# Two scan chunks a step instead of three in a MetaFormer kernel with selective scans

## The chip, the cores and the metric

The kernel runs on one NeuronCore of a Trainium2 chip, as one launch. The metric is the device time of that core in microseconds (us), the median over several executions. Everything is float32.

## The reference

An image batch of 4 x 384 channels x 32 x 32 positions goes through two layers, each with a token mixer and a feed-forward part. Both mixers are selective scans (state-space models). In layer 0 the 1024 positions of an image are read in four directions (rows, columns, and both backwards); in layer 1 in one direction, but with 768 channels. What costs the time is this recurrence, for each channel `d` and each of 16 states `n`:

```python
dA = jnp.exp(dtt[..., None] * A)
h = h * dA + (dtt * ut)[..., None] * bt[:, :, None, :]
y = jnp.einsum('bkdn,bkn->bkd', h, ct)
```

`dt` is a softplus of a low-rank projection, `bt` and `ct` are projections of the input that have one row per state and position, and `A` is negative. Around the scans lie layer norms, a small feed-forward part as a Kronecker product (layer 0), input and output projections, a causal convolution of four taps and a SiLU gate (layer 1), and at the end a layer with four experts, of which each token takes two.

## The kernel before

The scan layers and the expert layer run one after the other. In `conv_layers`, work is divided into **passes**. A pass is one image, one direction (layer 0) or one group of 384 channels (layer 1), and one half of the positions, T = 512 columns. Layer 0 has 8 passes an image, layer 1 has 4: 48 passes for four images. Of the two passes over the halves of one sequence, the first starts from zero and keeps its last states (`keep_state`), the second starts from these.

Within a pass there are 384 channels x 16 states, so 48 scans of 128 partitions x 512. A partition holds one channel and one state: the upper 64 partitions hold state 2m, the lower 64 state 2m + 1, of the same 64 channels. `dts` and `dtus` hold dt and dt x u doubled that way, 64 channels to a chunk, six chunks to a pass. They are filled by DMAs from `dt` and `dtu` (`prep_pass`). A **step** takes three of the six chunks (`part` 0 or 1) and one pair of states (m = 0 to 7): 16 steps a pass, 768 in all. A step consists of:

- the loads of the rows for b and c, two DMAs of 64 partitions each into the rings `bts` and `cts` of three tiles (`load`, L849), issued on SP's queue;
- one product on POOL, `s = dtus x b`, 128 x 1536 (`times_b`, L855), into the ring `ss` of five tiles;
- three decays on ACT, `da = exp(a x dt)`, into three PSUM banks `das`, bank x for chunk x (`decay`, L861);
- three scans on DVE (`scan`, L870). A scan writes over `da` in PSUM or over `s` in SBUF;
- the products with c: for scans that ended in PSUM on DVE (`times_c`, L902), for those in SBUF on POOL (`times_c_pool`, L913). `share[i]` says how many of the three stay with DVE: 1, 2 or 3;
- three matmuls on PE that add the two states of a channel and sum over the steps into `acc` (`add`, L889). With `both` as 128 x 64 weights, each writes 64 partitions, the upper or the lower half of the array's columns by the chunk's number. Chunks 0 and 1 of a step are issued as one entry, chunk 2 as an entry of its own.

At the end of a pass `gather` takes `acc` into the result (L472 to L485, L680).

Nothing of this order is found by hardware: the class `Plan` plays the engines through with fixed costs, while it emits the instructions. Main streams (the steps) have fixed orders for each engine; **side jobs** (layer norms, projections, convolution, feed-forward, softplus, one serial chain of them) are put into the streams where a main instruction is not due, and `choose` says which goes first. `split` sets `share[i]` from how far ahead POOL is. `LOAD` (3.0 us) stands for a DMA; SP is taken to be free again after 0.1 us. Each engine then executes its list in order, with semaphores between engines.

Side jobs on ACT that need another function table reload it and go back (`SWITCH`): the softplus of each pass (L393), GELU (L495, L551) and SiLU (L638, L704).

After the scan layers, `moe_layer` keeps PE busy with the experts (L1200, L1212).

Of the kernel before, what the change touches and what calls it, by code (L numbers as in the profile page):

```python
# [17 lines left out]
P = 128  # L18
# [6 lines left out]
T = 512  # L25
# [193 lines left out]
def conv_layers(ctx, tc, ins, x2, const):  # L219
# [34 lines left out]
    dts = tiles(2, [P, NC, T], "dts")  # L254
    dtus = tiles(2, [P, NC, T], "dtus")
# [3 lines left out]
    NSR, NBR, NCR = 5, 3, 3  # L259
    ss = tiles(NSR, [P, NC, T], "s")  # L260
    bts = tiles(NBR, [P, T], "bt")
    cts = tiles(NCR, [P, T], "ct")
    state = sp.tile([P, NS, NC], F32, name="state")
# [4 lines left out]
    das = tiles(NC, [P, T], "da", pool=ps_1)  # L268
# [98 lines left out]

    def until(*keys):

        while not all(k in plan.end for k in keys):  # L370
            yield None
        return max(plan.end[k] for k in keys)

    def prep_pass(q, p, h, u, u_view):


        nr = q["rank"]
        for c in range(NC):
            pd = yield from ps.take(True)
            yield PE, 0.95  # L380
            nc.tensor.matmul(  # L381
                pd,
                lhsT=q["dtw"][QROW : QROW + nr, c * P : (c + 1) * P],
                rhs=q["xd"][QROW : QROW + nr, cols(h)],
                start=True,
                stop=True,
            )
            bias = pv(q["dtb"], q["c0"] + c, 1)
            yield ACT, 0.65
            nc.scalar.activation(dt[:, c, :], pd, AF.Identity, bias=bias)  # L390
            ps.give(pd)
        yield ACT, 1.45 + SWITCH
        nc.scalar.activation(dt, dt, AF.Softplus)  # L393
        exp_set()
        for c in range(NC):
            yield POOL, 1.35
            nc.gpsimd.tensor_tensor(u_view(dtu[:, c, :]), u_view(dt[:, c, :]), u[:, c], ALU.mult)
        for part in range(2):
            before = 0.0
            if p:  # L400
                before = yield from until(("scan", NS * (p - 1) + 8 * part + 7, 2))
            for to, of in ((dts[part], dt), (dtus[part], dtu)):
                yield SP, LOAD, before
                for side in range(2):

                    mine = [x for x in range(NC) if (3 * part + x) % 2 == side]
                    chunks = [(3 * part + x) // 2 for x in mine]
                    for k in range(2):
                        nc.sync.dma_start(
                            out=to[k * HP : (k + 1) * HP, mine[0] : mine[-1] + 1 : 2, :],  # L410
                            in_=of[side * HP : (side + 1) * HP, chunks[0] : chunks[-1] + 1, :],
                        )
            plan.end["pass", p, part] = plan.now + LOAD + 2.0
# [419 lines left out]
    steps = [(p, n) for p in range(len(passes)) for n in range(NS)]  # L833
# [11 lines left out]
    def load(i, of, ring):  # L845
        p, part, m = place(i)
        for k in range(2):
            row = of + 2 * m + k
            nc.sync.dma_start(  # L849
                out=ring[i % len(ring)][k * HP : (k + 1) * HP, :],  # L850
                in_=quad(p)["rows"][row : row + 1, cols(passes[p][4])].partition_broadcast(HP),
            )

    def times_b(i):
        nc.gpsimd.tensor_tensor(ss[i % NSR], dtus[place(i)[1]], rep(bts[i % NBR]), ALU.mult)  # L855

    def decay(i, x):
        p, part, m = place(i)
        q = quad(p)
        g = 2 * q["c0"] + 3 * part + x  # L860
        nc.scalar.activation(das[x], dts[part][:, x, :], AF.Exp, scale=q["a"][:, g, m : m + 1])  # L861

    def scan(i, x):
        p, j = steps[i]
        _, _, _, _, _, first, rev = passes[p]
        way = slice(None, None, -1) if rev else slice(None)
        s = ss[i % NSR][:, x, way]
        d = das[x][:, way]
        in_psum = x < share[i] if x else True
        nc.vector.tensor_tensor_scan(  # L870
            d if in_psum else s, d, s, 0.0 if first else state[:, j, x : x + 1], ALU.mult, ALU.add
        )
        if not in_psum:
            plan.skip.add(("mult", i, x))
            plan.end["da free", i, x] = plan.free[DVE]

    def keep_state(i, of):

        p, j = steps[i]
        at = 0 if passes[p][6] else T - 1  # L880
        for x in (0, 1) if of == 0 else (2,):
            src = das[x] if x < share[i] else ss[i % NSR][:, x, :]
            nc.vector.tensor_copy(state[:, j, x : x + 1], src[:, at : at + 1])  # L883

    def add(i, xs):
        _, part, m = place(i)
        for x in xs:
            c, side = divmod(3 * part + x, 2)
            nc.tensor.matmul(  # L889
                acc[side * HP : (side + 1) * HP, c, :],  # L890
                lhsT=both,
                rhs=ss[i % NSR][:, x, :],
                start=m == 0,
                stop=m == NS // 2 - 1,
            )
# [5 lines left out]
    def times_c(i, x):  # L901
        nc.vector.tensor_tensor(ss[i % NSR][:, x, :], das[x], cts[i % NCR], ALU.mult)  # L902
        plan.end["split", i] = 0.0
        plan.end["part", i, x] = plan.end["da free", i, x] = plan.end["mult", i, x]
        if x == 2:
            plan.end["c", i] = plan.end["mult", i, 2]
        elif share[i] == NC:
            plan.skip.add(("c", i))

    def times_c_pool(i):  # L910
        m = share[i]
        s = ss[i % NSR]
        nc.gpsimd.tensor_tensor(s[:, m:, :], s[:, m:, :], rep(cts[i % NCR], NC - m), ALU.mult)  # L913
        for x in range(m, NC):
            plan.end["part", i, x] = plan.end["c", i]

    STEP, C1, SPARE = 4.8, 1.24, 6.0
    share = dict.fromkeys(range(N), 2)
    main, gathers, decays, bs, cs, bl, cl = ([] for _ in range(7))
    adds = [[], []]  # L920
    AT = (0.0, 1.18, 3.6)
    for i in range(N):
        p, part, m = place(i)
        first = passes[p][5]
        after = ("state", i, 1) if first else ("scan", i, 2)
        ring = [("add", i - NSR, k) for k in range(2)] if i >= NSR else []
# [6 lines left out]
                [rows] + ([("mult", i - NCR, 0), ("part", i - NCR, 1), ("c", i - NCR)] if i >= NCR else []),  # L933
# [3 lines left out]
        bs.append(Op(("b", i), 3.42, [("pass", p, part), ("bt", i), *ring], lambda i=i: times_b(i)))  # L937
        for x in range(NC):
            free = [("da free", i - 1, x)] if i else []
            decays.append(Op(("da", i, x), 0.63, [("pass", p, part), *free], lambda i=i, x=x: decay(i, x)))  # L940
        for x in (0, 1, "state 0", "mult 0", "mult 1", 2, "state 1", "mult 2"):
            if isinstance(x, int):
                cost = 1.12 if first else 1.18
                op = Op(("scan", i, x), cost, [("da", i, x), ("b", i)], lambda i=i, x=x: scan(i, x))
            elif x.startswith("state"):
                k = int(x[-1])
                op = Op(("state", i, k), 0.14 - 0.07 * k, [], lambda i=i, k=k: keep_state(i, k))
                if not first:
                    continue
            else:  # L950
                k = int(x[-1])
                op = Op(("mult", i, k), 0.62, [("ct", i)], lambda i=i, k=k: times_c(i, k))
            main.append(op)
        cs.append(Op(("c", i), C1, [("ct", i), after, ("split", i)], lambda i=i: times_c_pool(i)))
        wait = [("gather", p - 1)] if m == 0 and p else []
        for k, xs in enumerate(((0, 1), (2,))):
            adds[k].append(
                Op(("add", i, k), 0.95, [("part", i, x) for x in xs] + wait, lambda i=i, xs=xs: add(i, xs))
            )
        if i % NS == NS - 1:  # L960
            gathers.append(
                Op(("gather", p), 2.0, [("add", n, k) for n in (i - 8, i) for k in range(2)], lambda p=p: gather(p))
            )

    def needed(plan, i, x):
# [4 lines left out]
        what, j, k = op.key  # L970
        y = AT[k] if what == "scan" else (2.36, 2.98, STEP)[k] if what == "mult" else (2.36, STEP)[k]
# [7 lines left out]
    def pool_choice(plan, mains, side):  # L979
# [3 lines left out]
        if 0 in by:  # L983
            t, op = by[0]
            d = plan.head(DVE, 1)
            late = (d.key[1] if d else N) - op.key[1] >= 2
# [14 lines left out]
    def split(plan, i, start):  # L1001
# [3 lines left out]
        if ahead - waiting < C1:  # L1005
            return NC
        return 1 if ahead - waiting > SPARE else 2

    def choose(plan, e, mains, side):
        if e == POOL:  # L1010
            return pool_choice(plan, mains, side)
        if e == DVE:
            for n, (t, k, op) in enumerate(mains):
                if op.key[0] == "scan" and op.key[2] == 1:
                    i = op.key[1]
                    share[i] = split(plan, i, t + 2.4)
                    plan.streams[POOL][0][i].cost = (0.0, 2.3, C1, 0.0)[share[i]]
# [7 lines left out]
        if e == ACT:  # L1025
# [3 lines left out]
            due = needed(plan, head.key[1], AT[head.key[2]]) - head.cost - LAG  # L1029
# [5 lines left out]
        if e == PE:  # L1035
            d, a = plan.head(DVE, 1), plan.head(PE, 1)
            behind = (d.key[1] if d else N) - (a.key[1] if a else N)
            if behind > 2 and best[0] <= start:
# [7 lines left out]
        {DVE: [gathers, main], ACT: [decays], POOL: [cs, bs], PE: adds, SP: [bl, cl]}, jobs, choose  # L1046
# [280 lines left out]
```

## Time and profile before

| what | us |
|---|---|
| runs shown | 6753.74, 6752.0, 6747.33 |
| median | 6752.0 |
| profiled execution, its own time | 6755.91 |
| its span in the profile | 6754.0 |
| last scan ends, from the span's start | about 4470 |
| DVE busy | 4145.4 (61%) |
| POOL busy | 4080.2 (60%) |
| ACT busy | 2735.4 (41%) |
| PE busy (overlapping matmuls counted once) | 5601.9 (83%) |

Shares over the whole span mean little, since two stages with different limits follow each other: up to about 4473 us the scans, from there on the end of the last side jobs and the expert layer. The profile names a group of instructions by its line, engine, operation and tiles, then gives their number, the time they kept the engine busy, the mean of one in ns, and the idle time just ahead of them with what ended it. A row `A <- B` of the waits is: A's engine stood idle until B was done; total us, number, longest.

### The profile page before, as it was taken

The page shows a single profiled execution, that of the slowest core. Times are in us where ns is not written, and L with a number is a line of the kernel's source. Part 1 is how long each engine was busy: PE and PEld are TensorE (multiplying, and loading weights), DVE is VectorE, ACT ScalarE, POOL GpSimd, SP SyncE. Part 2 cuts the span into 40 slices and gives each one's busy share as a digit, 9 for nine tenths or more (in the row PEclk, how much of TensorE's full clock was granted, in tenths as well). Part 3 has the DMA queues.
Part 4 walks back from the last instruction along what each step waited for, and adds up shares of the span by engine and source line. Part 5 has one row for each costly group of instructions (what it writes and reads, how often), then busy time and mean ns, then how long its engine had stood idle before and what let it go on. Part 6 is the DMA issues. An engine that isn't in the chain of part 4 may idle for free. (4 is left out here: it accounts for less than half of the span.)

```text
span 6754.0 us, 47474 instructions
## 1 busy us (share of the span) xinstructions
PE 5601.9 (83%) x12352; PEld 1929.1 (29%) x12352; DVE 4145.4 (61%) x5421; ACT 2735.4 (41%) x3911; POOL 4080.2 (60%) x1735
## 2 busy tenths in 40 slices
PE   6666789767777876878886897767899999999999
PEld 1111123112122211222221222223444444444444
DVE  6999989998889999899999885951100000000000
ACT  4444565555455645555555554432211111111111
POOL 6999888998889888999899875950000000000000
PEclk8787889887888988888887888888999999999999
DMA  4444444444445444445444433422000000000000
GB/s 130 143 140 143 138 119 141 143 134 124 133 139 159 136 132 139 130 144 157 144 142 138 118 109 106 148 88 105 0 0 0 28 0 8 21 0 0 10 14 14
DMA packets 413489, 644.55 MB, mean 95 GB/s; under 512 B 75104, under 2 KB 119200, under 8 KB 413216
## 3 DMA queue, kind: packets, MB, share of 16 engines
q1 hardware_dynamic: 413216, 641.52, 31.6%
q8 instruction: 97, 1.59, 0.1%
q14 instruction: 176, 1.44, 0.1%
HBM read 468.77 MB, written 21.50 MB: 73 GB/s over the span
## 5 line engine op out<-in xcount | busy, mean ns | idle before, releaser
L855 POOL TENSOR_TENSOR s<-dtus,bt 128x1536 f32<-128x1536 f32 x768 | 2640.6, 3447 | 177.6 <-PE acc L889 94.6
L889 PE MATMUL acc<-s,both 128*64 128x512 f32 x4608 | 2030.3, 742 | 838.1 <-POOL s L913 547.2
L861 ACT ACTIVATE da<-dts,a 128x512 f32<-128x512 f32 x2304 | 1511.2, 683 | 1469.2 <-DVE s L902 1305.7
L1226 POOL TENSOR_TENSOR xb<-xb,yg 128x1536 f32<-128x1536 f32 x32 | 118.8, 3712 | 1834.3 <-DVE yg L1223 1775.4
L1223 DVE SCALAR_TENSOR_TENSOR yg<-py,pvt,gate 128x512 f32<-128x512 f32 x96 | 66.2, 746 | 1848.8 <-PE py L1200 1846.6
L913 POOL TENSOR_TENSOR s<-s,ct 128x512 f32<-128x512 f32 (+1 forms) x673 | 1044.8, 1554 | 207.6 <-DVE state L883 54.4
L889 PEld LDWEIGHTS acc<-s,both 128*64 128x64 f32 x4608 | 483.7, 156 | 2323.9 <-POOL s L913 985.7
L1200 PE MATMUL py<-hid,w 128*128 128x512 f32 x2304 | 1046.2, 592 | 1.5 <-DVE yg L1223 1.5
L1212 PE MATMUL ph<-tb,w 128*128 128x512 f32 x2304 | 1046.3, 592 | 0.0
L870 DVE TENSOR_TENSOR_SCAN da<-da,s 128x512 f32<-128x512 f32 x736 | 871.4, 1219 | 169.3 <-POOL s L855 101.0
L870 DVE TENSOR_TENSOR_SCAN da<-da,state,s 128x512 f32<-128x512 f32 x720 | 889.3, 1273 | 100.0 <-ACT da L861 90.3
L902 DVE TENSOR_TENSOR s<-da,ct 128x512 f32<-128x512 f32 x1456 | 944.0, 682 | 10.9 <-DMA ct<-rows 6.2
L1216 ACT ACTIVATE hid<-ph,pvt 128x512 f32<-128x512 f32 x384 | 263.9, 687 | 1523.2 <-PE ph L1212 1516.9
L1200 PEld LDWEIGHTS py<-hid,w 128*128 128x128 f32 x2304 | 437.7, 190 | 553.9 <-issue 550.4
L1212 PEld LDWEIGHTS ph<-tb,w 128*128 128x128 f32 x2304 | 438.0, 190 | 552.2 <-issue 551.9
L870 DVE TENSOR_TENSOR_SCAN s<-da,state,s 128x512 f32<-128x512 f32 x432 | 550.4, 1274 | 15.8 <-ACT da L861 15.8
L870 DVE TENSOR_TENSOR_SCAN s<-da,s 128x512 f32<-128x512 f32 x416 | 503.8, 1211 | 18.1 <-ACT da L861 17.9
L591 PE MATMUL ps<-u,w 128*128 128x512 f32 x576 | 294.8, 660 | 35.9 <-DMA w<-in_w_in_dram 29.0
L381 PE MATMUL ps<-xd,dtw 12*128 12x512 f32 (+1 forms) x288 | 188.8, 749 | 32.7 <-ACT dt L390 24.5
L543 PE MATMUL ps<-t,w 32*128 32x512 f32 x192 | 148.4, 904 | 40.8 <-DMA w<-in_w_fc_dram 38.6
L591 PEld LDWEIGHTS ps<-u,w 128*128 128x128 f32 x576 | 114.9, 209 | 219.1 <-issue 171.9
L724 PE MATMUL ps<-yx,w 128*128 128x512 f32 x288 | 144.6, 655 | 38.9 <-DMA w<-in_w_out_dram 36.4
(134 smaller groups left out, 3278.1 us busy)
## 6 DMA issues: line engine op xcount, KB each, us to landing
bt<-rows SPq DMA_DIRECT2D x1536, 128.0 KB, 3.0
ct<-rows SPq DMA_DIRECT2D x1536, 128.0 KB, 3.0
dts<-dt SPq DMA_DIRECT2D x192, 256.0 KB, 3.9
dtus<-dt SPq DMA_DIRECT2D x192, 256.0 KB, 3.4
dts<-dt SPq DMA_DIRECT2D x192, 128.0 KB, 3.2
dtus<-dt SPq DMA_DIRECT2D x192, 128.0 KB, 3.5
w<-in_w_dram SPq DMA_DIRECT2D x8, 2304.0 KB, 23.9
w<-in_w_in_dram SPq DMA_DIRECT2D x48, 192.0 KB, 3.0
```

The costliest lines, as they stand in the source:

```text
L381: nc.tensor.matmul(pd, lhsT=q["dtw"][QROW : QROW + nr, c * P : (c + 1) * P], rhs=q["xd"][QROW : QROW + nr, cols(h)], start=True, stop=True,)
L543: nc.tensor.matmul(ph[h], lhsT=w[:32, j, :], rhs=z[h][:32], start=True, stop=True)
L591: nc.tensor.matmul(pi, lhsT=w[:, c, :], rhs=u[:, c, cols(h)], start=c == 0, stop=c == NC - 1)
L855: nc.gpsimd.tensor_tensor(ss[i % NSR], dtus[place(i)[1]], rep(bts[i % NBR]), ALU.mult)
L861: nc.scalar.activation(das[x], dts[part][:, x, :], AF.Exp, scale=q["a"][:, g, m : m + 1])
L870: nc.vector.tensor_tensor_scan(d if in_psum else s, d, s, 0.0 if first else state[:, j, x : x + 1], ALU.mult, ALU.add)
L889: nc.tensor.matmul(acc[side * HP : (side + 1) * HP, c, :], lhsT=both, rhs=ss[i % NSR][:, x, :], start=m == 0, stop=m == NS // 2 - 1,)
L902: nc.vector.tensor_tensor(ss[i % NSR][:, x, :], das[x], cts[i % NCR], ALU.mult)
L913: nc.gpsimd.tensor_tensor(s[:, m:, :], s[:, m:, :], rep(cts[i % NCR], NC - m), ALU.mult)
L1200: nc.tensor.matmul(py[:, m, :], lhsT=w2[:, f, m * P : (m + 1) * P], rhs=hid, start=f == 0, stop=f == NF - 1,)
L1212: nc.tensor.matmul(ph, lhsT=w1[:, c, f * P : (f + 1) * P], rhs=ts[i][:, c, :], start=c == 0, stop=c == NC - 1)
L1216: nc.scalar.activation(hid, ph, AF.Gelu, bias=pv("b1", e * NF + f))
```

## The change

A step now takes two chunks, both 64-channel halves of one 128-channel chunk `c`, so that a pass has three groups of eight steps: 24 a pass, 1152 in all. With that:

- `times_b` is a product of 128 x 1024; `dts` and `dtus` become three tiles of two chunks, reloaded one by one when the last scan on them is done, by 24 DMAs of 64 partitions x 512 a pass (16 before, half of them twice as large).
- the rows for b and c are loaded for each of the 24 steps.
- `ss` has seven tiles of two chunks (14 chunks; five of three before); the rings for rows keep three tiles.
- the three PSUM banks `das` are used in rotation, bank (2i + x) mod 3, and no longer one for each chunk.
- `share[i]` is 1 or 2: the first scan's product is always DVE's, the second goes to POOL or stays.
- an `add` always issues two matmuls, one to each half of the columns.
- the order on DVE is scan 0, scan 1, (states), products; before, the products of chunks 0 and 1 stood ahead of scan 2.
- the planner's constants are set to the new step, and the thresholds at which POOL's product with c and PE's sums count as late go from 2 to 3 steps.

```diff
-    dts = tiles(2, [P, NC, T], "dts")
-    dtus = tiles(2, [P, NC, T], "dtus")
+    dts = tiles(NC, [P, 2, T], "dts")
+    dtus = tiles(NC, [P, 2, T], "dtus")
...
-    NSR, NBR, NCR = 5, 3, 3
-    ss = tiles(NSR, [P, NC, T], "s")
+    NSR, NBR, NCR = 7, 3, 3
+    ss = tiles(NSR, [P, 2, T], "s")
...
-    das = tiles(NC, [P, T], "da", pool=ps_1)
+    NDA = 3
+    das = tiles(NDA, [P, T], "da", pool=ps_1)
...
-        for part in range(2):
+        for c in range(NC):
             before = 0.0
             if p:
-                before = yield from until(("scan", NS * (p - 1) + 8 * part + 7, 2))
-            for to, of in ((dts[part], dt), (dtus[part], dtu)):
+                before = yield from until(("scan", NJ * (p - 1) + 8 * c + 7, 1))
+            for to, of in ((dts[c], dt), (dtus[c], dtu)):
                 yield SP, LOAD, before
...
+                for x in range(2):
                     for k in range(2):
...
+                        nc.sync.dma_start(out=to[k * HP : (k + 1) * HP, x, :], in_=of[x * HP : (x + 1) * HP, c, :])
...
     def times_b(i):
-        nc.gpsimd.tensor_tensor(ss[i % NSR], dtus[place(i)[1]], rep(bts[i % NBR]), ALU.mult)
+        nc.gpsimd.tensor_tensor(ss[i % NSR], dtus[place(i)[1]], rep(bts[i % NBR], 2), ALU.mult)
+
+    def bank(i, x):
+        return das[(2 * i + x) % NDA]
...
-    def add(i, xs):
-        _, part, m = place(i)
-        for x in xs:
-            c, side = divmod(3 * part + x, 2)
+    def add(i):
+        _, c, m = place(i)
+        for x in range(2):
             nc.tensor.matmul(
-                acc[side * HP : (side + 1) * HP, c, :],
+                acc[x * HP : (x + 1) * HP, c, :],
                 lhsT=both,
                 rhs=ss[i % NSR][:, x, :],
...
     def times_c_pool(i):
-        m = share[i]
-        s = ss[i % NSR]
-        nc.gpsimd.tensor_tensor(s[:, m:, :], s[:, m:, :], rep(cts[i % NCR], NC - m), ALU.mult)
...
+        s = ss[i % NSR][:, 1, :]
+        nc.gpsimd.tensor_tensor(s, s, cts[i % NCR], ALU.mult)
+        plan.end["part", i, 1] = plan.end["c", i]
...
-    STEP, C1, SPARE = 4.8, 1.24, 6.0
-    share = dict.fromkeys(range(N), 2)
+    STEP, C1 = 3.15, 1.24
+    share = dict.fromkeys(range(N), 1)
...
+        for x in range(2):
+            k = 2 * i + x - NDA
+            free = [("da free", k // 2, k % 2)] if k >= 0 else []
+            decays.append(Op(("da", i, x), 0.63, [("pass", p, c), *free], lambda i=i, x=x: decay(i, x)))
...
-            late = (d.key[1] if d else N) - op.key[1] >= 2
+            late = (d.key[1] if d else N) - op.key[1] >= 3
...
-        if ahead - waiting < C1:
-            return NC
-        return 1 if ahead - waiting > SPARE else 2
+        return 2 if ahead - waiting < C1 else 1
```

More of the change, by code (lines that the diff above doesn't have):

```diff
@@ L258, in conv_layers @@
     wxs = tiles(2, [P, NC, QROW + R0], "wx")
-    NSR, NBR, NCR = 5, 3, 3
-    ss = tiles(NSR, [P, NC, T], "s")
+    NSR, NBR, NCR = 7, 3, 3
+    ss = tiles(NSR, [P, 2, T], "s")
     bts = tiles(NBR, [P, T], "bt")
     cts = tiles(NCR, [P, T], "ct")
-    state = sp.tile([P, NS, NC], F32, name="state")
+    state = sp.tile([P, 8 * NC, 2], F32, name="state")
     tmp = Free(tiles(3, [P, NC, T], "tmp"))
@@ L365, in rows_out @@
         nc.sync.dma_start(out=q["rows"], in_=q["xd"][: 2 * NS, :])
+    NJ = 8 * NC
     def until(*keys):
@@ L397, in prep_pass @@
             nc.gpsimd.tensor_tensor(u_view(dtu[:, c, :]), u_view(dt[:, c, :]), u[:, c], ALU.mult)
-        for part in range(2):
+        for c in range(NC):
             before = 0.0
             if p:
-                before = yield from until(("scan", NS * (p - 1) + 8 * part + 7, 2))
-            for to, of in ((dts[part], dt), (dtus[part], dtu)):
+                before = yield from until(("scan", NJ * (p - 1) + 8 * c + 7, 1))
+            for to, of in ((dts[c], dt), (dtus[c], dtu)):
                 yield SP, LOAD, before
-                for side in range(2):
-                    mine = [x for x in range(NC) if (3 * part + x) % 2 == side]
-                    chunks = [(3 * part + x) // 2 for x in mine]
+                for x in range(2):
                     for k in range(2):
[L409 to L413, printed above, removed]
+                        nc.sync.dma_start(out=to[k * HP : (k + 1) * HP, x, :], in_=of[x * HP : (x + 1) * HP, c, :])
+            plan.end["pass", p, c] = plan.now + LOAD + 1.0
     def prep0(b):
@@ L831, in conv_layers @@
         jobs.append((key, deps + ([chain[n - 1][0]] if n else []), 1000 + n, phases))
-    steps = [(p, n) for p in range(len(passes)) for n in range(NS)]
+    steps = [(p, j) for p in range(len(passes)) for j in range(NJ)]
     N = len(steps)
@@ L845, in load @@
     def load(i, of, ring):
-        p, part, m = place(i)
+        p, c, m = place(i)
         for k in range(2):
@@ L854, in times_b @@
     def times_b(i):
-        nc.gpsimd.tensor_tensor(ss[i % NSR], dtus[place(i)[1]], rep(bts[i % NBR]), ALU.mult)
+        nc.gpsimd.tensor_tensor(ss[i % NSR], dtus[place(i)[1]], rep(bts[i % NBR], 2), ALU.mult)
+    def bank(i, x):
+        return das[(2 * i + x) % NDA]
     def decay(i, x):
-        p, part, m = place(i)
+        p, c, m = place(i)
         q = quad(p)
-        g = 2 * q["c0"] + 3 * part + x
-        nc.scalar.activation(das[x], dts[part][:, x, :], AF.Exp, scale=q["a"][:, g, m : m + 1])
+        g = 2 * (q["c0"] + c) + x
+        nc.scalar.activation(bank(i, x), dts[c][:, x, :], AF.Exp, scale=q["a"][:, g, m : m + 1])
     def scan(i, x):
@@ L867, in scan, with keep_state @@
         s = ss[i % NSR][:, x, way]
-        d = das[x][:, way]
-        in_psum = x < share[i] if x else True
+        d = bank(i, x)[:, way]
         nc.vector.tensor_tensor_scan(
-            d if in_psum else s, d, s, 0.0 if first else state[:, j, x : x + 1], ALU.mult, ALU.add
+            d if x < share[i] else s, d, s, 0.0 if first else state[:, j, x : x + 1], ALU.mult, ALU.add
         )
-        if not in_psum:
+        if x >= share[i]:
             plan.skip.add(("mult", i, x))
             plan.end["da free", i, x] = plan.free[DVE]
-    def keep_state(i, of):
+    def keep_state(i):
         p, j = steps[i]
         at = 0 if passes[p][6] else T - 1
-        for x in (0, 1) if of == 0 else (2,):
-            src = das[x] if x < share[i] else ss[i % NSR][:, x, :]
+        for x in range(2):
+            src = bank(i, x) if x < share[i] else ss[i % NSR][:, x, :]
             nc.vector.tensor_copy(state[:, j, x : x + 1], src[:, at : at + 1])
-    def add(i, xs):
-        _, part, m = place(i)
-        for x in xs:
-            c, side = divmod(3 * part + x, 2)
+    def add(i):
+        _, c, m = place(i)
+        for x in range(2):
             nc.tensor.matmul(
-                acc[side * HP : (side + 1) * HP, c, :],
+                acc[x * HP : (x + 1) * HP, c, :],
                 lhsT=both,
@@ L901, in times_c @@
     def times_c(i, x):
-        nc.vector.tensor_tensor(ss[i % NSR][:, x, :], das[x], cts[i % NCR], ALU.mult)
+        nc.vector.tensor_tensor(ss[i % NSR][:, x, :], bank(i, x), cts[i % NCR], ALU.mult)
         plan.end["split", i] = 0.0
         plan.end["part", i, x] = plan.end["da free", i, x] = plan.end["mult", i, x]
-        if x == 2:
-            plan.end["c", i] = plan.end["mult", i, 2]
-        elif share[i] == NC:
+        if share[i] == 2:
             plan.skip.add(("c", i))
+            plan.end["c", i] = plan.end["mult", i, x]
     def times_c_pool(i):
-        m = share[i]
-        s = ss[i % NSR]
-        nc.gpsimd.tensor_tensor(s[:, m:, :], s[:, m:, :], rep(cts[i % NCR], NC - m), ALU.mult)
-        for x in range(m, NC):
-            plan.end["part", i, x] = plan.end["c", i]
-    STEP, C1, SPARE = 4.8, 1.24, 6.0
-    share = dict.fromkeys(range(N), 2)
-    main, gathers, decays, bs, cs, bl, cl = ([] for _ in range(7))
-    adds = [[], []]
-    AT = (0.0, 1.18, 3.6)
+        s = ss[i % NSR][:, 1, :]
[3 more added lines that the diff above has]
+    share = dict.fromkeys(range(N), 1)
+    main, gathers, decays, bs, cs, bl, cl, adds = ([] for _ in range(8))
     for i in range(N):
-        p, part, m = place(i)
+        p, c, m = place(i)
         first = passes[p][5]
-        after = ("state", i, 1) if first else ("scan", i, 2)
-        ring = [("add", i - NSR, k) for k in range(2)] if i >= NSR else []
+        after = ("state", i) if first else ("scan", i, 1)
         rows = ("quad", p if first else p - 1)
@@ L932, in conv_layers @@
                 LOAD,
-                [rows] + ([("mult", i - NCR, 0), ("part", i - NCR, 1), ("c", i - NCR)] if i >= NCR else []),
+                [rows] + ([("part", i - NCR, x) for x in range(2)] if i >= NCR else []),
                 lambda i=i: load(i, 0, cts),
@@ L936, in conv_layers @@
         )
[L937 to L953, printed above, removed]
+        ring = [("add", i - NSR)] if i >= NSR else []
@@ new lines, in conv_layers @@
+        bs.append(Op(("b", i), 2.33, [("pass", p, c), ("bt", i), *ring], lambda i=i: times_b(i)))
+        for x in range(2):
+            k = 2 * i + x - NDA
+            free = [("da free", k // 2, k % 2)] if k >= 0 else []
+            decays.append(Op(("da", i, x), 0.63, [("pass", p, c), *free], lambda i=i, x=x: decay(i, x)))
+            main.append(
+                Op(("scan", i, x), 1.12 if first else 1.18, [("da", i, x), ("b", i)], lambda i=i, x=x: scan(i, x))
+            )
+        if first:
+            main.append(Op(("state", i), 0.14, [], lambda i=i: keep_state(i)))
@@ L954, in conv_layers @@
+        for x in range(2):
+            main.append(Op(("mult", i, x), 0.6, [("ct", i)], lambda i=i, x=x: times_c(i, x)))
         cs.append(Op(("c", i), C1, [("ct", i), after, ("split", i)], lambda i=i: times_c_pool(i)))
         wait = [("gather", p - 1)] if m == 0 and p else []
[L956 to L963, printed above, removed]
+        adds.append(Op(("add", i), 0.95, [("part", i, 0), ("part", i, 1), *wait], lambda i=i: add(i)))
@@ L965, in needed @@
+        if i % NJ == NJ - 1:
+            gathers.append(Op(("gather", p), 2.0, [("add", i - 8 * k) for k in range(NC)], lambda p=p: gather(p)))
     def needed(plan, i, x):
@@ L969, in needed @@
             return plan.free[DVE]
-        what, j, k = op.key
-        y = AT[k] if what == "scan" else (2.36, 2.98, STEP)[k] if what == "mult" else (2.36, STEP)[k]
+        what, j, *k = op.key
+        y = 1.18 * k[0] if what == "scan" else 2.36 if what == "state" else 2.36 + 0.6 * k[0]
         return max(plan.free[DVE], plan.now) + (i - j) * STEP + x - y
@@ L1015, in choose @@
                     i = op.key[1]
-                    share[i] = split(plan, i, t + 2.4)
-                    plan.streams[POOL][0][i].cost = (0.0, 2.3, C1, 0.0)[share[i]]
+                    share[i] = split(plan, i, t + 1.2)
         best = min(mains, key=lambda x: (x[0], x[1])) if mains else None
@@ L1028, in choose @@
                 return side_of
-            due = needed(plan, head.key[1], AT[head.key[2]]) - head.cost - LAG
+            due = needed(plan, head.key[1], 1.18 * head.key[2]) - head.cost - LAG
             if best and best[0] <= start and not aged:
@@ L1035, in choose @@
         if e == PE:
-            d, a = plan.head(DVE, 1), plan.head(PE, 1)
+            d, a = plan.head(DVE, 1), plan.head(PE, 0)
             behind = (d.key[1] if d else N) - (a.key[1] if a else N)
-            if behind > 2 and best[0] <= start:
+            if behind > 3 and best[0] <= start:
                 return main_of
@@ L1045, in conv_layers @@
     plan = Plan(
-        {DVE: [gathers, main], ACT: [decays], POOL: [cs, bs], PE: adds, SP: [bl, cl]}, jobs, choose
+        {DVE: [gathers, main], ACT: [decays], POOL: [cs, bs], PE: [adds], SP: [bl, cl]}, jobs, choose
     )
```

## The prediction

> **What bounds the kernel now.** I read the table by windows first, cut where the work changes: the start (to 83 us), seven passes with hardly any other work, the long mixed stretch, a gap, the last four passes, and the expert layer.
>
> ```profile
> 83.00:659.00 576.00, 382.49 (x758) 91.82 (x756) 563.64 (x757) 269.70 (x389) 557.78 (x241) 0.80 0.48 143
> 659.00:4043.00 3384.00, 2670.70 (x5717) 752.04 (x5718) 3080.89 (x3980) 1855.09 (x2681) 3017.53 (x1270) 0.84 0.46 136
> 4043.00:4126.00 83.00, 61.39 (x124) 22.03 (x122) 0.49 (x2) 35.37 (x43) 7.61 (x5) 0.85 0.22 61
> 4473.00:6754.00 2281.00, 2183.70 (x5132) 976.06 (x5132) 139.72 (x202) 367.90 (x510) 156.01 (x66) 0.97 0.05 17
> ```
>
> The columns are the window, its length, then PE, PEld, DVE, ACT and POOL busy, clock, DMA share and GB/s. In the clean passes DVE is busy for 563.64 of 576 us (98%) and POOL for 557.78 (97%): the two are full together. In the mixed stretch they are 91% and 89% full. From 4043 to 4126 both stand, because the last layer's input is not ready: the chain of side jobs sets that point. The last 2281 us are the expert layer, which the change does not touch. So the changed code can move about 4,390 us, and there two engines set the pace almost equally. Next, what they spend it on (the groups, shapes kept apart):
>
> ```profile
> L855 POOL TENSOR_TENSOR s<-dtus,bt 128x1536 f32<-128x1536 f32 x768 | 2640.6, 3447 | 177.6 <-PE acc L889 94.6 <-issue 35.5 <-DMA dtus<-dt 16.5
> L902 DVE TENSOR_TENSOR s<-da,ct 128x512 f32<-128x512 f32 x1456 | 944.0, 682 | 10.9 <-DMA ct<-rows 6.2 <-issue 1.1 <-PE ps L543 0.7
> L913 POOL TENSOR_TENSOR s<-s,ct 128x512 f32<-128x512 f32 x498 | 633.8, 1273 | 140.1 <-issue 36.5 <-DVE state L883 29.4 <-DVE s L870 25.6
> L913 POOL TENSOR_TENSOR s<-s,ct 128x1024 f32<-128x1024 f32 x175 | 411.0, 2353 | 67.6 <-DVE state L883 24.9 <-DVE s L870 19.7 <-issue 12.2
> ```
>
> Last, the waits, and one place where ACT holds DVE up:
>
> ```profile
> DVE da L870 <- ACT da L861: 158.3, 99, 6.0
> DVE da L870 <- POOL s L855: 104.1, 9, 82.5
> DVE s L870 <- ACT da L861: 33.7, 18, 4.3
> ```
> ```profile
> 408.26 1.28 ACT L393 ACT_TABLE_LOAD   x1
> 409.55 1.48 ACT L393 ACTIVATE dt<-dt 128x1536 f32<-128x1536 f32 x1
> 411.06 1.28 ACT L239 ACT_TABLE_LOAD   x1
> 412.35 1.30 ACT L861 ACTIVATE da<-dts,a 128x512 f32<-128x512 f32 x2
> ```
> ```profile
> 413.14 2.35 DVE L870 TENSOR_TENSOR_SCAN da<-da,s 128x512 f32<-128x512 f32 x2 [1.15 <-ACT da L861]
> ```
>
> DVE waits 192 us for decays (158.3 + 33.7) and practically never for POOL (82.5 of the 104.1 us is the gap at 4043). The timeline shows why: a softplus with its two table loads keeps ACT for 4.09 us, and the next decay comes 1.15 us late.
>
> **What the Trainium skill says.** "GPSIMD Engine Reference", section 3.1 Elementwise, gives a two-input product a cost per element and a fixed dispatch per instruction. The trace agrees: 1273, 2353 and 3447 ns for 512, 1024 and 1536 elements, so about 1.09 us per 512 and 0.19 us fixed. "SBUF — State Buffer", section Who interferes with whom: a DVE instruction with at most one SBUF input does not contend with GpSimd. Scans and products take their other input from PSUM, and both engines do run 97% full with unchanged durations; the change keeps that. "TensorE: Matmul & The Clock Gate", Part 3, lets matmuls on different columns run together. Twelve records of L889 at 2012.97 take 3.65 us, 0.30 each, against 0.43 for L1200 (5.15 us for 12 in the chain), which fits pairs that overlap.
>
> **The change part by part**, by counts from both programs' instruction lists.
>
> *POOL.* 768 products with b of 1536 become 1152 of 1024. The same shape in L913 takes 2353 ns: 1152 x 2.353 = 2711 us, less 2640.6, is +70 (384 more fixed costs). Products with c become 911 of 512, 911 x 1.273 = 1160, less 633.8 + 411.0, is +115. POOL: **+185 us**.
>
> *DVE.* Scans stay 2304 and state copies 1152. Products fall from 1456 to 1393: 63 x 0.648 (944.0/1456) = -41. In passes that keep states, three scans and copies take 3.82 us now (the lone scan is followed at once by its copy and drained), while two with their copies take 2.49, both read in the timeline near 1530 us, so 1.5 x 2.49 = 3.74: -0.085 for each of 384 steps, -33. DVE work: **-74 us**.
>
> *ACT.* The 2304 decays stay, the banks rotate over three. I reckon how long ACT may be away without a late decay, with a scan at 1.18 us, a product at 0.6 and a decay at 0.67. Now, after decay 2 (done 0.67 into a step of 4.72), decay 0 of the next step must start by 4.05: 3.4 us. Afterwards a step lasts 2.96; decay 1 needs the bank that the product ending the step before frees, then decay 0 of the next step follows at once (done at 1.34), and the next decay 1 must start by 2.96 + 0.51: 2.1 us. Absences with table loads number 90 in both lists; 72 follow decay 2 now, 78 follow decay 0 afterwards. Each costs 1.25 us more: +112. Bounds: nothing if POOL has DVE waiting anyway, +170 if absences without table loads suffer too. I take **+112**.
>
> *PE.* A sum alone takes 2 x 0.43 = 0.86 us, a pair estimated the same; 768 singles vanish into pairs: 768 x 2 x 0.86 less 1152 x 0.86 = 330 us of PE time. PE sets nothing here; what is released by sums on DVE is the gathers (some 46 us of waits). I take -15, bounds 0 and -46.
>
> *SP.* Row loads rise from 3072 to 4608, chunk loads from 768 to 1152 smaller ones:
>
> ```profile
> 201.42 1.19 SPq L849 DMA_DIRECT2D bt<-rows  x2
> 202.70 1.18 SPq L849 DMA_DIRECT2D ct<-rows  x2
> 203.98 1.18 SPq L849 DMA_DIRECT2D bt<-rows  x2
> 1514.28 3.31 SPq L409 DMA_DIRECT2D dts<-dt  x4
> 1517.63 3.34 SPq L409 DMA_DIRECT2D dtus<-dt  x4
> ```
>
> Back to back, a pair takes 1.28 us. In a clean pass of 82 us SP issues 16 x 2 x 1.28 = 41 us of rows and two batches of 6.8, so 55 us (67%). Afterwards it is 24 x 2 x 1.28 = 61 plus three batches of eight loads at about 0.65 each, 5.2, so 77 us (some 93%). SP is in order, so rows behind a batch come up to 5.2 us late. They have slack: b's row may load once the product three steps back is done, and at 3.45 us a step there are 3 x 3.45 - 2.35 = 8.0 us, against some 3.7 for issue (0.6) and landing (3.0 in the DMA table). A batch just exceeds the 4.3 left. I take +20, bounds 0 and +216 (144 batches x 1.5).
>
> *Sum.* DVE changes by -74 + 112 = +38, POOL by +185. A product costs 0.648 on one and 1.273 on the other, so if the planner's split keeps both full, the pace moves by (1.273 x 38 + 0.648 x 185)/1.921 = **+88**, between the +38 of DVE alone and the +185 of POOL alone. Of 48 passes the four ahead of the gap are covered by the side chain: 44/48 of 88 is +80. With PE -15 and SP +20: **+85**. The profiled execution took 6755.9 us (span 6754.0 and 1.9 around it), so 6841; the median of the runs is 3.9 lower, so 6837, which I round to **6840**.
>
> **The rivals.**
> 1. *Faster: DVE alone sets the pace.* POOL's 185 us fit into its idle 366 us of the mixed stretch (3384 - 3017.5), and rotating banks let decays run ahead, so ACT adds nothing: (-74 - 20) x 44/48 = -86, 6666. For it: DVE hardly waits for POOL now. Against: the clean passes, where POOL has 3% left and needs more. It decides if extra ACT waits stay under 40 us; half of it gives about 6710.
> 2. *POOL sets the pace.* Everything added there lengthens the passes: 185 x 44/48 = +170, 6922. For it: a clean pass then holds 24 x 2.353 + 17 x 1.273 + 3 x 1.40 = 82.3 us of POOL work, against 82.3 us that a pass lasts now. Against: POOL has slack in mixed passes.
> 3. *SP's queue falls behind*, rows are late at each batch: +216 above half of the main sum, about 7010.
> 4. *The change does little of what it says*: the sums already mostly overlap with other sums, and the finer steps only trade fixed costs for banks; within 0.2%, 6752.
>
> **How the numbers follow.** Chances: main case 0.45, POOL 0.17, SP 0.13, the faster case 0.19, no difference 0.06. A measurement of this kernel tells about 0.2% (14 us) from no change. Faster 0.19, same 0.06, slower 0.75. The range 6690 to 6990 leaves out the outer half of the faster case and most of SP's. The main case alone spans 6780 to 6910.
>
> **What would show it.** The b product should read about 2353 ns x1152, and POOL's busy time in the passes rise by some 185 us. DVE's waits for decays should rise from 192 towards 300 us. In clean passes POOL should be 98% busy, a pass lasting 83 to 84 us. SP's waits for POOL should shrink from over 1000 us. I am wrong if waits for decays fall, or if DVE or POOL waits chiefly for bt or ct loads.

## The result and the profile after

The changed kernel takes 6952.05 us (median; 6947.94 to 6954.93) against 6749.66 for the kernel before in the same comparison: a ratio of 1.0304, 95% interval 1.0286 to 1.0322. It is slower by 3%, some 202 us, where 1.3% (6840) was forecast. The direction held and the range too, but the size was off by more than a factor of two.

The page's groups, with the columns of before (line, engine, operation, tiles, shapes, number, busy us, mean ns, idle time just ahead and what ended it):

```profile
L852 POOL TENSOR_TENSOR s<-dtus,bt 128x1024 f32<-128x1024 f32 x1152 | 2708.6, 2360 | 177.4 <-DMA bt<-rows 120.7
L908 POOL TENSOR_TENSOR s<-s,ct 128x512 f32<-128x512 f32 x911 | 1157.8, 1272 | 279.9 <-DMA ct<-rows 85.5
L899 DVE TENSOR_TENSOR s<-da,ct 128x512 f32<-128x512 f32 x1393 | 927.2, 680 | 266.0 <-DMA ct<-rows 258.8
```

The instructions cost what was forecast: 2708.6 us for b (2711), 1157.8 for c on POOL (1160). What is new is what ends the idle time: loads of rows, on both engines. The prediction had named that as a sign of being wrong. Ahead of DVE's products there were 10.9 us of idle time before, now 266.0. The waits of DVE (engine and line, for whom, total us, times, longest):

```profile
DVE s L899 <- DMA ct<-rows: 258.8, 123, 6.1
DVE s L869 <- ACT da L861: 204.9, 90, 4.6
DVE da L869 <- ACT da L861: 43.7, 22, 5.2
```

And of POOL:

```profile
POOL s L852 <- DMA bt<-rows: 120.7, 84, 4.3
POOL s L908 <- DMA ct<-rows: 85.5, 41, 4.2
```

The same by windows, cut at the starts of the same passes in both kernels (seven clean passes, then 36 mixed ones; columns as in the prediction). Before:

```profile
154.20:720.30 566.10, 379.52 (x751) 91.74 (x750) 554.52 (x711) 266.69 (x384) 553.14 (x237) 0.79 0.48 144
720.30:3947.80 3227.50, 2540.40 (x5416) 712.07 (x5417) 2935.58 (x3827) 1779.98 (x2548) 2886.45 (x1214) 0.84 0.46 137
```

After:

```profile
154.70:789.60 634.90, 388.13 (x756) 83.97 (x757) 549.57 (x707) 262.87 (x384) 569.33 (x312) 0.76 0.59 175
789.60:4164.50 3374.90, 2542.32 (x5443) 677.31 (x5441) 2892.26 (x3781) 1785.01 (x2569) 3011.71 (x1694) 0.82 0.60 175
```

A clean pass now lasts 634.9/7 = 90.7 us, not the 83 to 84 forecast and not the 80.9 of before. But neither engine is fuller: DVE fell from 98% to 87%, POOL from 98% to 90%. So no engine's work sets this pace; both wait. One place in the timeline shows for what (SPq rows are DMA issues on SP's queue):

```profile
395.37 1.27 POOL L908 TENSOR_TENSOR s<-s,ct 128x512 f32<-128x512 f32 x1
396.63 2.46 SPq L409 DMA_DIRECT2D dts<-dt  x4
399.14 3.77 SPq L409 DMA_DIRECT2D dtus<-dt  x4
399.25 1.26 DVE L869 TENSOR_TENSOR_SCAN s<-da,state,s 128x512 f32<-128x512 f32 x1
403.02 2.45 SPq L846 DMA_DIRECT2D ct<-rows  x4
406.59 0.69 DVE L899 TENSOR_TENSOR s<-da,ct 128x512 f32<-128x512 f32 x1 [6.08 <-DMA ct<-rows]
```

A batch of eight chunk loads holds SP from 396.63 until after 402.9; that is a long one, the median of 138 such batches is 5.04 us. The rows for c behind it are issued from 403.02, and the first pair has landed by 406.59. Meanwhile DVE has done its scans by 400.51 and stands for 6.08 us. This is the rival that the prediction gave a chance of 0.13, SP's queue behind its batches. The experiments had to tell whether it carries the loss, or whether the waits only fall where an engine would have waited anyway.

### The profile page after: what moved, and what is told of

The parts are those of the page before. It is cut to its first block, busy times and chain, and to the rows that moved or that the text cites. A ratio compares the mean times of both kernels' runs of the same rounds, so it can differ in the third digit from the quotient of the medians.

```text
span 6953.2 us, 52355 instructions
## 1 busy us (share of the span) xinstructions
PE 5575.8 (80%) x12352; PEld 1871.6 (27%) x12352; DVE 4083.0 (59%) x5358; ACT 2726.2 (39%) x3911; POOL 4237.8 (61%) x2357
## 5 line engine op out<-in xcount | busy, mean ns | idle before, releaser
L852 POOL TENSOR_TENSOR s<-dtus,bt 128x1024 f32<-128x1024 f32 x1152 | 2708.6, 2360 | 177.4 <-DMA bt<-rows 120.7
L886 PE MATMUL acc<-s,both 128*64 128x512 f32 x4608 | 1967.5, 767 | 1052.5 <-POOL s L908 504.4
L908 POOL TENSOR_TENSOR s<-s,ct 128x512 f32<-128x512 f32 x911 | 1157.8, 1272 | 279.9 <-DMA ct<-rows 85.5
L886 PEld LDWEIGHTS acc<-s,both 128*64 128x64 f32 x4608 | 417.5, 160 | 2534.7 <-POOL s L908 984.7
L899 DVE TENSOR_TENSOR s<-da,ct 128x512 f32<-128x512 f32 x1393 | 927.2, 680 | 266.0 <-DMA ct<-rows 258.8
L869 DVE TENSOR_TENSOR_SCAN da<-da,s 128x512 f32<-128x512 f32 x686 | 826.7, 1219 | 99.9 <-POOL s L852 75.7
L869 DVE TENSOR_TENSOR_SCAN s<-da,s 128x512 f32<-128x512 f32 x466 | 559.7, 1201 | 134.3 <-ACT da L861 134.1
L384 PE MATMUL ps<-xd,dtw 12*128 12x512 f32 (+1 forms) x288 | 218.8, 851 | 26.0 <-ACT dt L393 12.3
L400 POOL TENSOR_TENSOR dt<-dt,u 128x512 f32<-128x512 f32 x96 | 133.5, 1404 | 54.1 <-ACT dt L396 54.1
```

What stands on the lines that cost most here:

```text
L384: nc.tensor.matmul(pd, lhsT=q["dtw"][QROW : QROW + nr, c * P : (c + 1) * P], rhs=q["xd"][QROW : QROW + nr, cols(h)], start=True, stop=True,)
L869: nc.vector.tensor_tensor_scan(d if x < share[i] else s, d, s, 0.0 if first else state[:, j, x : x + 1], ALU.mult, ALU.add)
L886: nc.tensor.matmul(acc[x * HP : (x + 1) * HP, c, :], lhsT=both, rhs=ss[i % NSR][:, x, :], start=m == 0, stop=m == NS // 2 - 1,)
L899: nc.vector.tensor_tensor(ss[i % NSR][:, x, :], bank(i, x), cts[i % NCR], ALU.mult)
L908: nc.gpsimd.tensor_tensor(s, s, cts[i % NCR], ALU.mult)
```

## Experiments

Times are medians, ratios are against the kernel before, timed along with them; the waits are from each kernel's waits view.

One limit holds for all but the last: a change of a ring, of the order of steps or of SP's costs makes the planner plan everything anew. In five pairs of versions compared instruction by instruction, 258 to 437 of the 1152 steps then have another split of the products with c, and side jobs stand elsewhere. A difference of a few tens of us may therefore not be the remedy's alone.

### A fourth tile for the rows of c

```diff
-    NSR, NBR, NCR = 7, 3, 3
+    NSR, NBR, NCR = 7, 3, 4
```

> The changed kernel with a ring of four tiles for the rows of c in place of three; b's ring stays at three. Theory A (SP's queue is late behind the chunk loads and the three-deep rings cannot cover it): a fourth tile gives ct one more step, some 3.5 us, so DVE's waits for ct fall from 259 us to under 80, POOL's from 86 to under 40, POOL's waits for bt (121) stay, and the time falls by 100 to 200 us, to 6750-6850. Theory B (POOL's 157 us of added work and the decays set the pace, and the waits for ct only fall where an engine would have waited anyway): the waits for ct fall as well, but waits for b or for decays take their place and the time stays within 40 us of 6952.

6798.18 us, ratio 1.0079 (1.0064 to 1.0094): three quarters of the loss is gone with one tile of 2 KB a partition (the new plan also moves 38 products with c from POOL to DVE).

```profile
DVE s L899 <- DMA ct<-rows: 63.5, 33, 4.5
POOL s L852 <- DMA bt<-rows: 165.2, 109, 5.7
```

DVE's waits for ct fall from 258.8 to 63.5 us; those of POOL for bt, expected to stay at 121, rise to 165.2. Theory B, by which the time would hardly move, is out.

### The same loads, in another order on SP

Every chunk load is entered in pieces of two DMAs, the planner counts 1.2 us of SP for each entry, and rows that are due go first.

```diff
-                self.free[e] = start + (0.1 if e == SP else cost)
+                self.free[e] = start + (1.2 if e == SP else cost)
...
-                yield SP, LOAD, before
                 for x in range(2):
+                    yield SP, LOAD, before
                     for k in range(2):
...
+        if e == SP:
+            return main_of if best[0] <= start else side_of
         return side_of if start <= best[0] else main_of
```

> The changed kernel with the same loads in another order on SP: each chunk load is entered in four pieces of two DMAs, the planner counts 1.2 us of SP for each piece and each pair of rows, and lets due rows go first. Rings, products and loads are the same in number. Theory A: rows no longer stand 5 to 6 us behind a batch, waits for ct and bt (259 + 121 + 86 us) fall by more than half, and the time falls by 100 to 200 us. Theory B: the time stays within 40 us of 6952. A third one, that SP is too busy as such (80% of its time goes into issuing): waits move but do not shrink by half, the gain is under 80 us.

6830.97 us, 1.0128 (1.0113 to 1.0143), with as many loads and rings as in the changed kernel. The waits for rows fall by two thirds:

```profile
DVE s L899 <- DMA ct<-rows: 100.0, 86, 3.8
POOL s L908 <- DMA ct<-rows: 32.2, 25, 4.9
POOL s L852 <- DMA bt<-rows: 15.7, 26, 1.4
```

The number of loads is the same, and so are the bytes that the DMA engines move; the order is worth 121 us here. The last scan starts at 4514 us (4668 in the changed kernel, 4469 before). After it, 34 us more pass than in the changed kernel (2319 against 2285). A likely reason is that the planner's 1.2 us for every load also slowed the side chain; in the versions below, which count them for rows and pieces alone, that stretch lasts 2290 to 2304 us.

### Fewer row loads

The first two chunks' steps alternate and share each load of rows: 3072 row DMAs as before the change, not 4608.

```diff
-        return p, j // 8, j % 8
+        return (p, j % 2, j // 2) if j < 16 else (p, 2, j - 16)
+
+    def row_of(i):
+
+        p, j = steps[i]
+        return 16 * p + (j // 2 if j < 16 else j - 8)
...
```

> The changed kernel with the steps of the first two chunks interleaved, so that both use one load of the rows: 16 loads of b and c a pass as in the kernel before, in place of 24 (3072 row DMAs, not 4608). Products, scans, decays and chunk loads are the same in number. Theory A: the rows' slack doubles for two thirds of a pass and SP falls from 80% to some 60% busy; waits for ct and bt fall from 466 us to under 150 and the time falls by 120 to 220 us, to 6730-6830. Theory B: within 40 us of 6952.

6942.84 us, 1.0292 (1.0276 to 1.0307). This expectation failed: SP's DMA instructions, counted with the gaps under 0.15 us between them, fill only 58% of the scan stage, as before the change (79% in the changed kernel), and still the time falls by 9 us only. With as many row loads as before the change, more DMA work is no explanation of the loss. SP's timeline shows why:

```profile
480.38 2.46 SPq L409 DMA_DIRECT2D dts<-dt  x4
482.88 2.53 SPq L409 DMA_DIRECT2D dtus<-dt  x4
485.51 3.74 SPq L855 DMA_DIRECT2D bt<-rows  x6
489.36 1.17 SPq L855 DMA_DIRECT2D ct<-rows  x2
```

and DVE's beside it:

```profile
493.61 1.29 DVE L908 TENSOR_TENSOR s<-da,ct 128x512 f32<-128x512 f32 x2 [6.80 <-DMA ct<-rows]
```

Two chunks now come free together, so two batches follow each other (the first fills 473.95 to 479.0, with one pair of rows between them), just where rows are again used by one step only. Sorted by step, DVE's waits for ct stand at steps 17 and 18 (176 us) and 0 (37 us), and nearly none among the first 16. So a queue that is 58% busy on average is late in bursts.

The same with the chunk loads in pieces (here only rows and pieces cost the planner SP time, other loads as before):

> The changed kernel with shared rows for the first two chunks (16 row loads a pass) and the chunk loads in pieces behind due rows; rings as in the changed kernel. Shared rows alone lowered SP from 79% to 58% busy and left the waits for ct at 238 us, as both chunks come free together and two batches follow each other. Theory A (bursts, not the mean load): with pieces the waits for rows fall below 150 us on both engines and the time falls by 150 to 240 us from 6943, to 6700-6790. If instead the order of the steps itself costs the time (single-use rows after shared ones): above 6860.

6757.87 us, 1.0014 (1.0008 to 1.0021): 185 us less with the same steps, rings and loads, from SP's order and the plan that follows from it. The three waits for rows fall from 422 us to 80. And with four tiles for c as well:

> As the last, with a ring of four tiles for the rows of c: the changed kernel with rows on time and no more row loads than before. Theory A: 6690-6730, at least level with the version of pieces and four tiles (6718), and 0.2 to 0.8% faster than the kernel before.

6732.01 us, 0.9981 (0.9973 to 0.9988): as expected against the kernel before, 0.2% faster, but slightly above its expected range and not level with the version that comes next.

### Both remedies in the changed kernel

> The changed kernel with both remedies: a ring of four for the rows of c, and the chunk loads entered in pieces of two DMAs behind due rows (here only rows and pieces are counted as 1.2 us of SP, other side jobs as before). Theory A (rows late behind bursts of chunk loads): waits for ct below 40 us and for bt below 60 us on both engines together, the time 20 to 60 us under that with four tiles alone (6798). Theory A2 (with rows on time the rest of the loss is POOL's added work and late decays): it stays at 6770-6800, some 30 to 50 us above the kernel before. Theory B (it is the longer issue lists, 80% of SP's time, whatever the order): no better than 6798.

6718.25 us, 0.9957 (0.9943 to 0.9972): 80 us under that with four tiles alone, more than theory A expected. The time of theory A2, above the kernel before, did not come. That does not make POOL's work and late decays free: the clean passes stay slower than before (82.7 us against 80.9), and something else outweighs it (see the side chain below).

Four tiles for b and c, six for s, loads in batches:

> The changed kernel with rings of four tiles for b and for c, and six tiles of s in place of seven to make room. The loads go out as in the changed kernel, in batches. Theory A: b's waits on POOL (186 us with c's ring alone at four) fall below 70 us and the time lies at or under 6798, by up to 60 us. If the shorter ring of s or the planner's split counts for more than b's rows: above 6798.

6777.51 us, 1.0052 (1.0036 to 1.0068); POOL's b products wait 13.4 us for their rows.

And with the pieces:

> The changed kernel with rings of four and four, six tiles of s, and the chunk loads in pieces behind due rows. Theory A: no waits for rows left to speak of (under 60 us in all); what remains of the loss is POOL's and ACT's part: 6750-6790. A time under 6735 would say that the change with rows on time is faster than the kernel before.

6713.71 us, 0.9955 (0.9939 to 0.9971), outside the 6750 to 6790 expected and under the 6735 named as the other outcome. **With rows on time the change is 0.4% faster than the kernel before.** The kernel before was not run with its three tiles and pieces; it waits little for rows (6.2 us ahead of DVE's products), but what pieces would bring there is open. What is left of waits on DVE:

```profile
DVE s L869 <- ACT da L861: 180.6, 78, 5.5
DVE da L869 <- ACT da L861: 93.6, 50, 4.1
```

This version and that of 6718.25 us beat both kernels; they cannot be told apart.

### The kernel before with less slack

```diff
-    NSR, NBR, NCR = 5, 3, 3
+    NSR, NBR, NCR = 5, 2, 2
```

> The kernel before with rings of two tiles for the rows of b and c in place of three. A row then has 2 x 5.7 - 3.4 = 8 us from the freeing of its tile to its use, about what the changed kernel leaves with three (3 x 3.5 - 2.4 = 8 us). Theory A: waits for ct and bt appear at the chunk loads, of which there are 96 batches here (144 there), and the time rises by 80 to 250 us. Theory B: three tiles were more than enough, rows are covered as before, and the time rises by less than 40 us.

6968.08 us, 1.0335 (1.0312 to 1.0357): the kernel before with a row's slack shortened by one of its longer steps is as slow as the changed kernel, with the same waits:

```profile
DVE s L902 <- DMA ct<-rows: 309.0, 135, 7.4
POOL s L855 <- DMA bt<-rows: 186.5, 79, 5.7
```

With its chunk loads in pieces:

> The kernel before with rings of two (6968) and its chunk loads in pieces of two DMAs behind due rows. Theory A: the waits for ct and bt there (309 + 191 us) come from the batches and fall by more than half, the time by 100 to 200 us, to 6770-6870. If two tiles are too few in themselves, without bursts: within 60 us of 6968.

6837.74 us, 1.0136 (1.0122 to 1.0150), waits for ct on DVE 141.1 us. About 130 of the 224 us go with the bursts, as expected; that the rest comes from two tiles being few was not tried further.

### POOL's fixed costs alone

```diff
-        nc.gpsimd.tensor_tensor(ss[i % NSR], dtus[place(i)[1]], rep(bts[i % NBR]), ALU.mult)
+        s, u = ss[i % NSR], dtus[place(i)[1]]
+        if i % 2:
+            nc.gpsimd.tensor_tensor(s[:, :2, :], u[:, :2, :], rep(bts[i % NBR], 2), ALU.mult)
+            nc.gpsimd.tensor_tensor(s[:, 2, :], u[:, 2, :], bts[i % NBR], ALU.mult)
+        else:
+            nc.gpsimd.tensor_tensor(s, u, rep(bts[i % NBR]), ALU.mult)
```

> The kernel before with the product with b of every second step issued as two, 128 x 1024 and 128 x 512: the same products, and 384 fixed costs of 0.19 us more on POOL, +73 us, which is what the changed kernel's b products add. The prediction priced POOL's work by the compromise of two full engines (about a third): +25 us. If POOL alone set the pace: +73. If DVE did and POOL's slack took it up: under +10.

6736.76 us, 0.9987 (0.9978 to 0.9996): POOL is busy for 4133.2 us in place of 4080.2, and the time does not rise; it is, if anything, 0.1% lower. That is the third of the outcomes named. The split of the products with c is the same (1456 stay with DVE). The first part of a split product is ready earlier, but that gives DVE little: its waits for POOL's product with b sum to 100.1 us in place of 104.1. The seven clean passes, to be compared with the first line of the windows of before:

```profile
153.60:720.90 567.30, 366.32 (x751) 89.90 (x751) 554.66 (x710) 266.61 (x384) 559.65 (x294) 0.79 0.48 143
```

POOL has 6.5 us more to do there, and they last 1.2 us longer: its slack took up most of it. In the profile the last four passes start 20 us earlier (4105.3 against 4125.5), for no reason that the runs show; that could hide a price of this size in the mixed stretch.

## Why the prediction was wrong in size

**SP: the step that failed.** The term was +20 us, with 0 to +216 as bounds. The fastest version, with rows on time, takes 6713.7, so lateness and what went with it cost about 238 us, more than the upper bound. Two parts of the step were right: the length of a batch (5.2 us forecast, 5.04 in the median), and the 3.7 us for issue and landing (3.6 in the place shown). Three things were wrong.

First, the step's own figures do not give 20: a batch of 5.2 us against 4.3 us of slack is 0.9 us late, and 144 times 0.9 is 130. No reason is given for taking less.

Second, I worked out the slack for a row of b (8.0 us) as an average and took it for c as well. A tile of c is freed only when the products of three steps back are done on DVE and on POOL (POOL was the last of the two in 898 of 1149 steps). Put together from the trace, step by step, a row of c has 8.6 us in the median from the freeing of its tile to the end of the scans, about what was reckoned, but in one step of ten it has less than 5.3 us (a row of b 7.0). In the place shown the tile is freed at 396.64 by POOL's product and DVE wants the new row at 400.51: 3.9 us, so nothing is left for a batch. That a single further tile for c brings 154 us agrees with it.

Third, I let a batch hit once; the rows that queue up behind it go out one pair after another at 1.28 us, so the next steps are late too (steps 0 and 1 after a pass's end wait 95 us in all, steps 16 and 17 wait 82).

The utilization was the wrong thing to look at. It was forecast as 93% in clean passes; it was 83% there in the changed kernel, 62% with shared row loads, where the waits were nearly the same, and 93% in the fastest version, which hardly waits. What the time follows is the waits for rows. Added up over DVE's waits for ct and POOL's for ct and bt, they are 465 us at 6952, 422 at 6943 (shared), 237 at 6798 (four tiles for c) and 47 at 6714; in the kernel before 19 at 6750, and 499 at 6968 with rings of two.

**POOL's work and its price.** The durations of POOL's instructions rose by 185 us, as forecast. Its busy time rose by 158 us (4080.2 to 4237.8), since instructions that follow each other overlap a little in the profile. But the price of that work, a third of it plus what the compromise gave, is not seen where it was tested: 53 us more on POOL did not slow the kernel before. The whole 158 us were not tested alone. That clean passes hold POOL 97% busy was no proof that it set the pace; the planner hands POOL what DVE leaves it time for. Here the first rival was nearer, in that POOL's slack takes up added work; that DVE alone sets the pace is not shown.

**DVE's work.** Forecast -74, busy time 4145.4 to 4083.0, -62. Nearly right.

**Late decays.** Forecast +112, measured 192 to 249 us, +57, and 274 with rows on time. The mechanism shows at a softplus: DVE waits 1.98 us now where it waited 1.15.

```profile
266.31 1.28 ACT L239 ACT_TABLE_LOAD   x1
```
```profile
268.33 1.23 DVE L869 TENSOR_TENSOR_SCAN da<-da,s 128x512 f32<-128x512 f32 x1 [1.98 <-ACT da L861]
```

That is 0.8 us more, not 1.25. Over the whole trace, DVE waits after 69 of the 90 absences with table loads (63 before), 165 us in all (101 before). So the reckoning had the right mechanism and took too much for each.

**PE.** The 768 single sums were to save 330 us of PE's time. In the profile PE's busy time for the sums fell from 2030.3 to 1967.5 us, 63 us: I let a single sum cost as much as a pair, though the sums before already overlapped for the most part, as the fourth rival says. The 15 us that the pace was to gain from it at the gathers fit: DVE's waits for sums there fell from 50 to 30 us.

**The side chain.** I let four passes count for nothing since the chain sets the start of the last layer. It does hold them up, but it moves: the last four passes start at 4125.5 us before and at 4083.9 in the fastest version. That is nearly all of that version's gain up to the last scan (4469.2 to 4425.8). Its clean passes are slower than before:

```profile
149.90:727.70 577.80, 373.80 (x754) 84.31 (x751) 553.94 (x716) 263.07 (x384) 557.32 (x304) 0.75 0.62 192
```

These are 11.7 us more over seven (566.1 before), or 82.5 us a pass, just under the 83 to 84 forecast. Why the chain is quicker there was not tried. The run with POOL's split products, which changes nothing else, moved the same point by 20 us, so part of the 0.4% may owe nothing to the finer step.

**Sum.** The main case's +85 was made of two terms that were too large (POOL, decays) and one far too small (SP). The direction was luck: it came true by the third rival's mechanism, and with that mechanism removed the same change is slightly faster.

## What to carry to other kernels

A finer step with the same ring depth shortens the time that each buffer covers; reckon the slack of every ring from its own last reader and for its tightest steps, not from the easiest ring and on average, and compare it with the longest burst in front of it on the issuing queue. The mean load of an in-order queue says little. When a planner takes a queue for free, count its issue time and cut bulk loads into pieces behind the loads that are due: here that, with one tile more, turned +3.0% into -0.4%.

## What was not expected of the hardware

In the changed kernel a row load of 64 partitions x 512 mostly holds SP for 444 to 600 ns (median 562 for b and 582 for c, longest 1810), and eight chunk loads hold it for 5.0 to 6.6 us. Issue on one queue alone, short gaps counted, filled 79% of the scan stage while the DMA engines were about 60% busy. And with DVE and POOL each 98% busy in the clean passes, 6.5 us more of POOL's work made them only 1.2 us longer.
